# Second stage's transfers issued from GpSimd's queue, first stage's layer 0 spread over all tiles, third stage's groups started one after another

## The chip, the cores and the metric

The kernel runs on one core of a Trainium2 chip. The core has five engines that run beside each other, each through its own list of instructions in order: TensorE (PE; its weight loads are listed as PEld), VectorE (DVE), ScalarE (ACT), GpSimd (POOL) and SyncE (SP), which computes nothing and issues transfers. Data lies in HBM (DRAM), in SBUF, and the results of matmuls in PSUM. The metric is the device time of one execution in microseconds (us); lower is better. Before the change it is 4272.32 us, the median of three runs (4270.29 to 4274.1).

## What is computed

Four graph layers run over 128 graphs of 128 nodes with 128 channels; each adds its result to x. `LN` is a layer normalisation over the channels, followed by a ReLU.

```python
h = relu(LN(x));  x = x + L0(h, adj)   # relation-typed mean of neighbours, norm, relu
h = relu(LN(x));  x = x + L1(h, adj)   # learned adjacency, below
h = relu(LN(x));  x = x + L2(h, adj)   # graph attention, 4 heads of 32
h = relu(LN(x));  x = x + L3(h, adj)   # graph attention, 1 head, elu
```

The costly part is layer 1, which looks at every pair of nodes of a graph:

```python
D = abs(x[:, :, None, :] - x[:, None, :, :])        # all pairs i, j
h = einsum('bijc,oc->bijo', D, W1) + b1             # 64 features a pair
h = (h - mean(h)) / sqrt(var(h) + EPS) * g1 + be1   # mean, var over ALL graphs and pairs
s = einsum('bijo,uo->biju', leaky(h), W2)[..., 0] + b2[0]
A = softmax(where(adj > 0, s, NEG), axis=-1)
y = einsum('bij,bjc->bic', A, x) @ Wg.T + bg
y = leaky(batchnorm(y))                             # again over all graphs
out = concatenate([x, y], axis=2) @ Wt.T + bt
```

The two normalisations over all graphs cut the work into three stages: no score can be computed before the features of all pairs are known, and no output before all y.

## The kernel before

Work is done in 32 groups of G = 4 graphs. The partitions are the nodes (or, for pair features, 2 x 64 features).

**Stage 1** does layer 0 and the pair features. `pairs(g)` takes a group's transposed `h`, and `pair_stats` goes through four tiles (`t`) of each of its four graphs (`k`), so a group has 16 tiles. For a tile, `pairwise` subtracts (line 164, output `d`; tiles 0 and 2 on DVE, 1 and 3, which are those in `ON_POOL`, on GpSimd), ACT takes the absolute value (166), PE multiplies with `w1T` (170, output `hp`), ACT copies to `hs` (182), and DVE takes statistics (183 to 190). `hs` goes to DRAM per graph (188). There are two `d` tiles for each of the two engines and two `hp` tiles. `layer0(g + 2)` runs beside `pairs(g)`: it is a generator of 13 pieces (loads; statistics; mask and degrees, lines 238 to 244; norm; two transposes; matmuls; sum; statistics; scale, 278; shift and add to x, 284, stored by 285; statistics; the norm for layer 1), each of the three norms with a power on GpSimd (116, 117). `_weave(main, side, steps)` takes `steps` pieces of the side work for each step of the main work, and what is left of it at the end. A program builder then orders the instructions of each engine by its own estimate, starting from the order in which the code issues them, and puts in the waits.

**Stage 2** reads the stored pair features back as z in halves of a graph, 1 MiB each (`fetch`, line 485; ten are fetched ahead, twelve buffers). `scores` normalises them (507 and 512 on ACT, 508 on DVE), multiplies by W2 (503) and copies out (519); `by_k` finishes a graph's scores (525, 529, 531) into `sk`. `to_rows` writes `sk` to a DRAM buffer `rows` with a skewed layout (538) and loads it back as `u` (541), which turns diagonals into rows. `finish1` loads x (547), normalises it (129, 140, output `hn`), transposes it (146), adds the two halves of u (556), does the softmax (555 to 574) and the matmuls (581 to 593), stores the new x (590) and y (596, into Z). In the loop, group g's scores run beside `finish1(g - 2)`. All of these transfers are issued from SP's queue, so one that waits for its data holds those behind it.

**Stage 3** does the rest of layer 1 and layers 2 and 3 per group (`group`, 30 steps): load (729 on), a first product (740), a norm, attention for two graphs at a time (757 to 762 into `pe`, softmax 690 to 700, transposes 146, product 777), a norm, layer 3's attention (795 to 812), store (820). Its tiles have three buffers, `x` four, `e` eight. `_round_robin` keeps three groups under way: it fills up to three, and gives each one step per turn. Since all groups have the same number of steps, three start together and end together.

Of the kernel before, what the change touches and what calls it, by code (L numbers as in the profile page):

```python
# [30 lines left out]
AHEAD = 2  # L31
# [9 lines left out]
def _weave(main, side, steps):  # L41


    due = 0.0
    for _ in main:
        due += steps
        while due >= 1:
            due -= 1
            next(side, None)
    for _ in side:  # L50
        pass


def _round_robin(works, at_once):

    flying = []
    while True:
        flying += list(itertools.islice(works, at_once - len(flying)))
        if not flying:
            return  # L60
        flying = [w for w in flying if next(w, works) is not works]


# [1 line left out]
def tile_gnn_stack(ctx: ExitStack, tc: tile.TileContext, a: dict, out: bass.AP):  # L65
    nc = tc.nc
    NB = a["x"].shape[0]
    NG = NB // G
# [6 lines left out]
    def big(name):  # L75
        return psum.tile([P, 2, 512], F32, tag="big", bufs=2, name=name)

    def sm(name):
        return psum.tile([P, G, P], F32, tag="sm", bufs=3, name=name)
# [23 lines left out]
    X = [dr.tile([P, G, P], F32, tag=f"x{g}", name=f"x{g}") for g in range(NG)]  # L103
    Z = [dr.tile([P, G, P], F32, tag=f"z{g}", name=f"z{g}") for g in range(NG)]
# [38 lines left out]
    def transpose(dst, src, func=AF.Copy):  # L143
        pt = sm("pt")
        for k in range(G):
            nc.tensor.transpose(pt[:, k, :], src[:, k, :], ident)  # L146
        nc.scalar.activation(dst, pt, func)  # L147

    def over_group(t):
        return t[:, None, :].to_broadcast([P, G, P])  # L150
# [42 lines left out]
    with tc.tile_pool(name="c0", bufs=1) as c0, tc.tile_pool(name="p0", bufs=2) as p0:  # L193
# [97 lines left out]
        def pairs(g):  # L291

            h = H1.pop(g)
            xp = psum.tile([P, G, P], F32, tag="xp", name="xp")
            for k in range(G):
                nc.tensor.transpose(xp[:, k, :], h[:, k, :], ident)
            xe = p0.tile([P, G, P + 2 * KH], F32, name="xe")
            nc.scalar.copy(xe[:, :, 0:P], xp)
            nc.scalar.copy(xe[:, :, P:], xp[:, :, 0:2 * KH])
            for k in range(G):  # L300
                yield from pair_stats(p0, xe, xp, k, g * G + k)
# [49 lines left out]
        with tc.If(nc.values_load(flag, min_val=0, max_val=1) > 0) as cmp, \  # L351
# [6 lines left out]
            for g in range(NG):  # L358
                x = pr.tile([P, G, P], F32, name="x")
# [36 lines left out]
            pass  # L396

        for g in range(NG):
            _weave(pairs(g), layer0(g + AHEAD) if g + AHEAD < NG else iter(()), 4)


    with tc.tile_pool(name="bn", bufs=1) as bn:
# [39 lines left out]
    with tc.tile_pool(name="c1", bufs=1) as c1, tc.tile_pool(name="p1", bufs=2) as p1:  # L442
# [26 lines left out]
        zero = c1.tile([P, G, ROW], F32, name="zero")  # L469
        nc.vector.memset(zero, 0.0)  # L470
        for n in range(2):
            rows = dr.tile([G, P, ROW], F32, tag=f"rows{n}", name=f"rows{n}")
            nc.sync.dma_start(rows.rearrange("g i r -> i g r"), zero)
            slots.append(rows)

        sk = []
# [11 lines left out]
        def next_z():  # L488
            z = fetched.pop(0)
            n = next(halves, None)  # L490
            if n is not None:
                fetched.append(fetch(n))
            return z

        def scores(k, s):

            ps = big("ps")[:, 0, :]

            def products(parts, j0):
                for i, (w, v) in enumerate(parts):  # L500
                    for c in range(4):
                        w0 = 31 - 2 * (j0 // 4)
                        nc.tensor.matmul(ps[32 * c:32 * c + 32, :], w[:, w0:w0 + 32], v[:, 512 * c:512 * c + 512],  # L503
                                         start=j0 == 0, stop=j0 > 0 and i == 1, skip_group_check=True)

            z0 = next_z()
            nc.scalar.activation(z0, z0, AF.Identity, bias=bias1, scale=scale1[:, 0:1])  # L507
            nc.vector.scalar_tensor_tensor(z0, z0, 0.01, z0, op0=OP.mult, op1=OP.max)  # L508
            yield
            z1 = next_z()  # L510
            zr = p1.tile([P, NT // 2 * KC * P], F32, name="zr", bufs=3)
            nc.scalar.activation(zr, z1, AF.Relu, bias=bias1, scale=scale1[:, 0:1])  # L512
            products([(w2z, z0)], 0)

            if behind:
                behind.pop()()
            products([(w2l, z1), (w2r, zr)], 4)
            su = p1.tile([P, 4, P], F32, name="su")
            nc.vector.tensor_copy(su.rearrange("p a b -> p (a b)"), ps)  # L519
            yield  # L520

            def by_k():
                pk = sm("pk")
                for kk in range(4):
                    nc.tensor.matmul(pk[:, kk, 0:16], su[:, kk, :], pick.rearrange("p h j -> p (h j)"),  # L525
                                     start=True, stop=True)

                out_k = s[:, k, 1:].rearrange("p (a b) -> p b a", b=4)
                nc.vector.tensor_tensor(out_k, pk[:, :, 0:16], add_k.rearrange("p h j -> p (h j)")[:, None, :]
                                        .to_broadcast([P, 4, 16]), OP.add)  # L530
                nc.vector.tensor_scalar(s[:, k, 2 * KH:], s[:, k, 2 * KH:], 0.5, None, op0=OP.mult)
            behind.append(by_k)

        def to_rows(g):

            rows = slots[g % 2]
            to = rows[0, 0, 0:1]
            nc.sync.dma_start(bass.AP(tensor=to.tensor, offset=to.offset,
                                      ap=[[ROW + 1, P], [P * ROW, G], [1, 1 + 2 * KH]]), sk[g % 2])
            u = p1.tile([P, G, ROW], F32, name="u")  # L540
            nc.sync.dma_start(u, rows.rearrange("g i r -> i g r"))
            return u

        def finish1(g, u):

            x = p1.tile([P, G, P], F32, name="x")
            nc.sync.dma_start(x, X[g])
            yield
            h = pre_norm(p1, x, MV1[:, g], RS1[:, g])
            yield  # L550
            hT = p1.tile([P, G, P], F32, name="hT")
            transpose(hT, h)
            yield
            cap = p1.tile([P, G, P], F32, name="cap")
            nc.vector.tensor_scalar(cap, M8[g], BIG, NEG12, op0=OP.mult, op1=OP.add)
            nc.vector.tensor_tensor(u[:, :, 0:2 * KH], u[:, :, 0:2 * KH], u[:, :, P:], OP.add)
            yield
            pt = sm("put")
            for k in range(G):
                nc.tensor.transpose(pt[:, k, :], u[:, k, 0:P], ident)  # L560
            yield
            e = p1.tile([P, G, P], F32, name="e1")
            nc.vector.tensor_tensor(e, u[:, :, 0:P], pt, OP.add)
            nc.vector.tensor_tensor(e, e, cap, OP.min)
            mx = small.tile([P, G], F32, name="mx")
            nc.vector.tensor_reduce(mx, e, AX.X, OP.max)
            yield
            nc.vector.tensor_tensor(e, e, mx[:, :, None].to_broadcast([P, G, P]), OP.subtract)
            nc.scalar.activation(e, e, AF.Exp)
            yield  # L570
            sums = small.tile([P, G], F32, name="sums")
            nc.vector.tensor_reduce(sums, e, AX.X, OP.add)
            nc.vector.reciprocal(sums, sums)
            nc.vector.tensor_tensor(e, e, sums[:, :, None].to_broadcast([P, G, P]), OP.mult)
            yield
            aT = p1.tile([P, G, P], F32, name="aT")
            transpose(aT, e)
            yield
            py = sm("py")
            for k in range(G):  # L580
                nc.tensor.matmul(py[:, k, :], h[:, k, :], aT[:, k, :], start=True, stop=True)
            yT = p1.tile([P, G, P], F32, name="yT")
            nc.scalar.copy(yT, py)
            yield
            po = sm("po")
            for kk in range(G):
                nc.tensor.matmul(po[:, kk, :], hT[:, kk, :], wtxT, start=True, stop=True)
            nc.vector.tensor_tensor(x, x, po, OP.add)
            nc.vector.tensor_tensor(x, x, over_group(bt), OP.add)
            nc.sync.dma_start(X[g], x)  # L590
            yield
            pz = sm("pz")
            nc.tensor.matmul(pz, wgT, yT, start=True, stop=True)
            y = p1.tile([P, G, P], F32, name="y")
            nc.scalar.activation(y, pz, AF.Identity, bias=bg)
            nc.sync.dma_start(Z[g], y)
            nc.vector.bn_stats(ST2[:, g, :], y.rearrange("p a b -> p (a b)"))

        def group_scores(g):
            for k in range(G):  # L600
                yield from scores(k, sk[g % 2])

# [25 lines left out]
    with tc.tile_pool(name="c2", bufs=1) as c2, tc.tile_pool(name="p2", bufs=3) as p2:  # L630
# [188 lines left out]
            nc.vector.scalar_tensor_tensor(x, ex, 1.0, x, op0=OP.min, op1=OP.add)  # L819
            nc.sync.dma_start(out[g * G:g * G + G].rearrange("b t c -> t b c"), x)  # L820

        _round_robin((group(g) for g in range(NG)), 3)


# [29 lines left out]
```

## Time and profile before

The profiled execution took 4268.02 us from the host's view of the device; its span, from the first to the last instruction, is 4266.1 us. The mean TensorE clock granted was 0.805.

| | PE | PEld | DVE | ACT | GpSimd |
|---|---|---|---|---|---|
| busy, us | 2964.6 | 1531.3 | 2913.5 | 2624.5 | 1419.4 |
| share of the span | 69% | 36% | 68% | 62% | 33% |

| stage | from, us | to, us | what marks it |
|---|---|---|---|
| 1 | 100 | 2101 | first and last `hp` matmul, line 170 |
| 2 | 2108 | 3215 | first fetch of z, line 485, to the sums over all y, line 621 |
| 3 | 3217 | 4266 | first `off`, line 736, to the end |

A row of busy times by window gives the window and its length, then for each engine the busy time and in brackets the number of instructions, then the granted clock of TensorE (1 is full speed), the busy share of the 16 transfer engines and GB/s. A row of waits gives the engine and the line that waited, what ended the wait, the total in us, the number of times and the longest. A timeline row gives start, duration, engine (SPq is SP's queue), line, operation, tiles, count, and in square brackets the idle time before it and what ended that.

In the whole profile every transfer but four runs through one queue, SP's, with 652 MB; no transfer is issued from GpSimd. `z<-hp` is 256 issues of 1 MiB with a median of 11.9 us to landing, `u<-rows` 5.6 us, `rows<-sk` 3.4 us, `x<-x` (loads and stores of all stages) 4.3 us.

### The profile page before, as it was taken

To read this page: it belongs to the slowest core of one execution; us is meant where nothing else is said; L and a number is where in the kernel's file an instruction comes from. 1 tells how busy PE (TensorE), PEld (TensorE's weight loads), DVE (VectorE), ACT (ScalarE), POOL (GpSimd) and SP (SyncE) were. 2 spreads that over 40 slices of the span, in tenths; PEclk is the share of its full clock that TensorE was granted. 3 is DMA by queue.
4 is the path that set the end of the run, shared out by engine and by line. 5 is a ranking of instruction groups with operands and counts; after the bars stand their busy time and mean duration, and the time that the engine had idled before them with its cause. 6 is when DMAs were issued, how large, how long until landed. Compare 5 with 4: busy or idle time off the path is not lost.

```text
span 4266.1 us, 43744 instructions
## 1 busy us (share of the span) xinstructions
PE 2964.6 (69%) x15142; PEld 1531.3 (36%) x15153; DVE 2913.5 (68%) x5971; ACT 2624.5 (62%) x3363; POOL 1419.4 (33%) x683
## 2 busy tenths in 40 slices
PE   1566666666657667666677677777777888888887
PEld 1222222222222222222123343333445666666665
DVE  5888888888888888877646666666665555555544
ACT  1677777777777777777755555555544554555544
POOL 2566666666666666556400000000001111111111
PEclk7788788888888878878877777777777888888877
DMA  6343333333333333333577777777751001000000
GB/s 205 121 170 156 136 156 155 133 158 153 143 148 153 153 138 153 150 128 160 220 295 288 298 303 294 278 289 302 305 183 45 23 29 39 23 23 23 21 16 15
DMA packets 182965, 659.12 MB, mean 155 GB/s; under 512 B 31312, under 2 KB 99792, under 8 KB 132560
## 3 DMA queue, kind: packets, MB, share of 16 engines
q1 hardware_dynamic: 182160, 652.04, 39.9%
q10 hardware_dynamic: 576, 4.19, 0.3%
q8 instruction: 123, 2.02, 0.2%
q14 instruction: 106, 0.87, 0.1%
HBM read 340.76 MB, written 315.42 MB: 154 GB/s over the span
## 4 chain that ended last, share of the span: by engine, by line
PE 42%; ACT 25%; DVE 10%; POOL 9%; DMA 7%; issue 5%; SPq 0%; POOLq 0%; DVEq 0%; ACTq 0%
PE hp L170 14%; ACT d L166 13%; POOL d L164 9%; ACT hs L182 6%; PE ps L503 5%; DMA x<-x 4%; PE pt L146 4%; PE pv L777 4%; PE pk L525 3%; PE pe L759 3%; DVE z L508 3%; PE pe L757 3%; DMA rows<-sk 2%; ACT e L700 2%; PE pr L718 2%
## 5 line engine op out<-in xcount | busy, mean ns | idle before, releaser
L170 PE MATMUL hp<-d,w1T 128*64 128x512 f32 x4096 | 1146.3, 706 | 691.4 <-ACT d L166 686.1
L164 POOL TENSOR_TENSOR d<-xe 128x2048 f32<-128x2048 f32 x256 | 1081.9, 4243 | 500.5 <-PE hp L170 463.9
L166 ACT ACTIVATE d<-d 128x2048 f32<-128x2048 f32 x512 | 968.7, 1921 | 307.3 <-POOL d L164 299.4
L170 PEld LDWEIGHTS hp<-d,w1T 128*64 128x64 f32 x4096 | 314.2, 161 | 1439.8 <-ACT d L166 862.3
L182 ACT COPY hs<-hp 128x1024 f32<-128x1024 f32 x512 | 516.1, 1021 | 216.6 <-PE hp L170 216.4
L164 DVE TENSOR_TENSOR d<-xe,xp 128x2048 f32<-128x2048 f32 x256 | 579.9, 2275 | 84.2 <-PE hp L170 84.2
L183 DVE BATCH_NORM_STATS2 st<-hs 128x6 f32<-128x512 f32 x512 | 350.0, 684 | 192.2 <-ACT hs L182 189.5
L507 ACT ACTIVATE z<-z,bias,scale 128x2048 f32<-128x2048 f32 x128 | 267.4, 2089 | 202.9 <-DMA z<-hp 191.2
L116 POOL TENSOR_SCALAR scale<-mv 128x1 f32<-128x1 f32 x1 | 0.2, 226 | 1106.7 <-DVE mv L621 1106.7
L116 POOL TENSOR_SCALAR lnrs<-lnmv 128x4 f32<-128x4 f32 x128 | 34.6, 270 | 962.9 <-DVE lnmv L124 962.9
L512 ACT ACTIVATE zr<-z,bias,scale 128x2048 f32<-128x2048 f32 x128 | 267.7, 2092 | 103.8 <-DMA z<-hp 71.4
L185 DVE BATCH_NORM_STATS2 st<-hs 128x6 f32<-128x512 f32 (+1 forms) x512 | 327.8, 640 | 0.0
L700 ACT ACTIVATE e<-e,mx 128x128 f32<-128x128 f32 x640 | 248.5, 392 | 86.1 <-DVE mx L697 84.8
L508 DVE SCALAR_TENSOR_TENSOR z<-z 128x2048 f32<-128x2048 f32 x128 | 292.3, 2285 | 12.3 <-ACT z L507 12.3
L147 ACT ACTIVATE hT<-pt 128x512 f32<-128x512 f32 x128 | 78.9, 616 | 325.4 <-PE pt L146 325.3
L691 DVE TENSOR_REDUCE mx<-e 128x4 f32<-128x512 f32 x160 | 104.7, 682 | 197.9 <-ACT e L690 196.7
L503 PE MATMUL ps<-z,w2z 128*32 128x512 f32 x1024 | 186.9, 812 | 56.6 <-DVE su L519 27.3
L146 PE MATMUL pt<-ident,e 128*128 128x128 f32 x768 | 150.7, 312 | 58.5 <-ACT e L700 23.0
L525 PEld LDWEIGHTS pk<-pick,su 128*128 128x128 f32 x1024 | 174.7, 256 | 37.5 <-DVE su L519 21.0
L777 PE MATMUL pv<-wr,eT 128*128 128x32 f32 x1024 | 168.0, 322 | 27.7 <-ACT eT L147 16.8
L146 PE MATMUL pt<-ident,hn 128*128 128x128 f32 x256 | 61.0, 358 | 179.5 <-DVE hn L140 179.5
L503 PE MATMUL ps<-z,w2l 128*32 128x512 f32 x1024 | 182.2, 794 | 0.4 <-DMA z<-hp 0.4
(190 smaller groups left out, 4784.2 us busy)
## 6 DMA issues: line engine op xcount, KB each, us to landing
hp<-hs SPq DMA_DIRECT2D x128, 2048.0 KB, 6.3
z<-hp SPq DMA_DIRECT2D x256, 1024.0 KB, 11.9
x<-x SPq DMA_DIRECT2D x128, 256.0 KB, 4.3
u<-rows SPq DMA_DIRECT2D x32, 384.0 KB, 5.6
x<-in_x_dram SPq DMA_DIRECT2D x32, 256.0 KB, 2.8
adj<-in_adj_dram SPq DMA_DIRECT2D x32, 256.0 KB, 4.6
agg<-a SPq DMA_DIRECT2D x32, 256.0 KB, 2.7
z<-y SPq DMA_DIRECT2D x32, 256.0 KB, 3.6
```

Source lines behind the costliest of these rows:

```text
L146: nc.tensor.transpose(pt[:, k, :], src[:, k, :], ident)
L164: eng.tensor_tensor(d, ahead, x[:, None, None, :].to_broadcast([P, 2, KC, P]), OP.subtract)
L166: nc.scalar.activation(d, d, AF.Abs)
L170: nc.tensor.matmul(hp[64 * hh:64 * hh + 64, c:c + 512], w1T, d[:, hh, c:c + 512], start=True, stop=True)
L182: nc.scalar.copy(hs[:, t, :], hp)
L183: nc.vector.bn_stats(st[:, 2 * t, :], hs[:, t, 0:512])
L185: nc.vector.bn_stats(st[:, 2 * t + 1, :], hs[:, t, 512:1024 - P * last])
L503: nc.tensor.matmul(ps[32 * c:32 * c + 32, :], w[:, w0:w0 + 32], v[:, 512 * c:512 * c + 512], start=j0 == 0, stop=j0 > 0 and i == 1, skip_g ...
L508: nc.vector.scalar_tensor_tensor(z0, z0, 0.01, z0, op0=OP.mult, op1=OP.max)
L525: nc.tensor.matmul(pk[:, kk, 0:16], su[:, kk, :], pick.rearrange("p h j -> p (h j)"), start=True, stop=True)
L700: nc.scalar.activation(e[:, q, :], e[:, q, :], AF.Exp, bias=mx[:, t, q:q + 1], accum_out=sums[:, t, q:q + 1])
L777: nc.tensor.matmul(pv[:, k - k0, hd, :], eT[:, hd, :], wr[:, k, 32 * hd:32 * hd + 32], start=True, stop=True)
```

## The change

Three things are edited.

1. `_weave` in stage 1 takes 0.75 steps of `layer0` per tile instead of 4. A group has 16 tiles, so 12 of the 13 pieces are taken within it and the last one after it.
2. In stage 2 the filling of `rows` with zeros, the store of `sk`, the load of `u`, the load and the store of x and the store of y are issued from GpSimd's queue (`nc.gpsimd.dma_start`). The fetches of z stay on SP's.
3. In stage 3 `_round_robin(..., 3)` becomes `_staggered(..., 10)`: a new group is started every ten turns, and all groups under way get one step per turn.

```diff
-def _round_robin(works, at_once):
+def _staggered(works, gap):

-    flying = []
+    flying, turn = [], 0
     while True:
-        flying += list(itertools.islice(works, at_once - len(flying)))
-        if not flying:
-            return
+        if turn % gap == 0 or not flying:
+            flying += list(itertools.islice(works, 1))
+            turn = 0
+            if not flying:
+                return
+        turn += 1
         flying = [w for w in flying if next(w, works) is not works]
...
-            _weave(pairs(g), layer0(g + AHEAD) if g + AHEAD < NG else iter(()), 4)
+            _weave(pairs(g), layer0(g + AHEAD) if g + AHEAD < NG else iter(()), 0.75)
...
-            nc.sync.dma_start(rows.rearrange("g i r -> i g r"), zero)
+            nc.gpsimd.dma_start(rows.rearrange("g i r -> i g r"), zero)
...
-            nc.sync.dma_start(bass.AP(tensor=to.tensor, offset=to.offset,
+            nc.gpsimd.dma_start(bass.AP(tensor=to.tensor, offset=to.offset,
                                       ap=[[ROW + 1, P], [P * ROW, G], [1, 1 + 2 * KH]]), sk[g % 2])
...
-            nc.sync.dma_start(u, rows.rearrange("g i r -> i g r"))
+            nc.gpsimd.dma_start(u, rows.rearrange("g i r -> i g r"))
...
-            nc.sync.dma_start(x, X[g])
+            nc.gpsimd.dma_start(x, X[g])
...
-            nc.sync.dma_start(X[g], x)
+            nc.gpsimd.dma_start(X[g], x)
...
-            nc.sync.dma_start(Z[g], y)
+            nc.gpsimd.dma_start(Z[g], y)
...
-        _round_robin((group(g) for g in range(NG)), 3)
+        _staggered((group(g) for g in range(NG)), 10)
```

## The prediction

> **What bounds the kernel now.** The kernel is three stages with barriers of data between them, so I cut the span first. The 40-slice rows and the first and last starts of the source-line view give stage 1 (lines 170 and below) to 2101 us, stage 2 (lines 485 to 597) to about 3215, stage 3 to 4266. Then I asked each stage for its busy time by window and for its waits.
>
> Stage 1: a window over one group of 128 `hp` matmuls each. The first line is a group that has a `layer0` woven in, the last two are the final groups, which have none left.
>
> ```profile
> 700.00:764.00 64.00, 41.96 (x168) 14.30 (x166) 52.14 (x99) 46.40 (x38) 40.16 (x16) 0.80 0.37 146
> 2003.00:2052.00 49.00, 33.37 (x132) 9.01 (x132) 38.44 (x52) 44.12 (x34) 32.92 (x9) 0.90 0.40 172
> 2052.00:2101.00 49.00, 32.01 (x130) 8.34 (x128) 39.10 (x53) 44.03 (x33) 33.33 (x8) 0.93 0.41 172
> ```
>
> [...]A group without `layer0` takes 49 us and ACT is 90% busy in it (44.1). With it a group takes 63.3 us on average (the fourth `hp` store of a group, line 188, leaves at 167.7 for the first group and at 2003.6 for the thirtieth: 1835.9 / 29) although no engine is over 83% busy: DVE gained 13.4 us of work and the group got 14 us longer. The work is added end to end, not beside.
>
> Stage 2, waits between 2250 and 3100 us, which are 25 groups:
>
> ```profile
> ACT z L507 <- DMA z<-hp: 168.0, 25, 7.9
> PE pt L146 <- DVE hn L140: 164.1, 26, 8.0
> DVE sk L529 <- PE pk L525: 132.5, 102, 2.8
> DVE u L556 <- DMA u<-rows: 129.2, 25, 6.4
> ```
>
> and of the queue SP alone:
>
> ```profile
> SPq L590 <- DVE x L589: 530.5, 25, 21.7
> ```
>
> Once per group ACT (for z), PE (for hn) and DVE (for u) all stand for 5 to 8 us. The SP line says why the fetches of z are late: for 21 us of each group SP stands at the store of line 590, with the fetches behind it. The timeline of one group shows the burst that follows:
>
> ```profile
> 2504.14 0.32 SPq L590 DMA_DIRECT2D x<-x  x1
> 2506.24 0.37 SPq L538 DMA_DIRECT2D rows<-sk  x1
> ...
> 2509.89 0.37 SPq L541 DMA_DIRECT2D u<-rows  x1
> 2510.32 0.50 SPq L547 DMA_DIRECT2D x<-x  x1
> 2510.86 4.46 SPq L485 DMA_DIRECT2D z<-hp  x7
> ...
> 2514.96 0.42 DVE L556 TENSOR_TENSOR u<-u 128x256 f32<-128x256 f32 x1 [4.70 <-DMA u<-rows]
> ...
> 2519.43 1.09 PE L146 MATMUL pt<-ident,hn 128*128 128x128 f32 x4 [5.53 <-DVE hn L140]
> ```
>
> The load of x (547) also stands behind line 541, which waits 3.6 us for `rows` to land. The period is about 33.2 us (line 538 at 2506.24, 2538.82, and so on over the stage).
>
> Stage 3: the timeline of SP (stores of three groups together), and a window over one such round.
>
> ```profile
> 4089.60 3.38 SPq L820 DMA_DIRECT2D out_dram<-x  x3
> 4184.21 3.38 SPq L820 DMA_DIRECT2D out_dram<-x  x3
> 4261.34 1.77 SPq L820 DMA_DIRECT2D out_dram<-x  x2
> ```
>
> ```profile
> 3380.00:3475.00 95.00, 78.30 (x448) 60.94 (x448) 51.38 (x156) 48.00 (x163) 12.49 (x15) 0.84 0.08 26
> ```
>
> Three groups in step take 95.5 us, the final two 74.1 (to 4261.3 from 4187.2, where the last store of the round before was issued). So one more group costs 21.4 us and 31 us per round are latency that all three stand through together. PE's waits in that round (`pt` for `h`, two of 4.3 and 5.3 us) are the normalisations, which all three reach at once. PE is at a mean clock of 0.84.
>
> [...] the windows around 5 to 8 us gaps show 0.50 and transposes take 1.09 us instead of 0.63.
>
> **Part by part.** The order in which the changed program's instructions stand was read beside the order of before; durations are those of before.
>
> *Layer 0 spread (4 to 0.75 steps per tile).* Nothing is added. In DVE's order the 14 us of `layer0` work, which stood in the first quarter of a group, now stand in two lumps of 6 to 8 us, and ACT's order alternates `d` and `hs` through two thirds of the group instead of half. Floor: DVE's 52.1 us. The undisturbed groups run at 90% of their busiest engine; 52.1 / 0.90 = 57.9 us. 63.3 - 57.9 = 5.4, over 30 groups 162 us. Ends: 11.2 x 30 = 336 (DVE never waits), and 0, or a loss of 2 us a group if GpSimd, where the power of the normalisation queues behind a 4.2 us `d`, holds DVE longer, three times per group, than the 75.2 us in 27 groups that the waits from 200 to 1900 us show (2.8 a group).
>
> *Second stage on GpSimd's queue.* GpSimd is idle there (its row shows 0 in slices 21 to 30). Per group five DMAs leave SP: rows, u, x, X, Z; SP keeps eight z fetches, which wait only for their slot. In DVE's account a group is 21.0 busy + 5.2 (u) + 5.3 (pk) + 1.1 (po) + 0.8 (rest) = 33.4. After: (a) x is now issued ahead of the wait for rows, and `hn` stands one group ahead of the transposes that use it, so PE's 6.3 us wait goes, and with it the half clock after it. DVE's wait for pk exists because PE is late; I take 2.0 of 5.3 as left (DVE still outruns PE at the fourth tile). (b) z is no longer behind line 590: ACT's 6.7 us wait goes. (c) u is late next: it still follows sk, rows and its own landing. Before it landed 8.9 us after sk[...]. On GpSimd the X and Z transfers stand between, but while rows lands. DVE's order has 6.0 us of work in that time (before 3.8): wait 3.7 instead of 5.2. Sum 33.2 - 3.3 - 1.5 = 28.4 us, 4.8 x 30 = 144 us. Ends: DMA share 0.78 of 33 is 25.8 us of full DMA, so at most 7.4 x 30 = 222; the other end is the slower rival. What GpSimd computes in stage 3 (powers, `off`) is behind the last stores only.
>
> *Third stage staggered.* The diff also starts a group every 10 steps instead of three together. A group has 30 steps, so three still fly, with the same buffers. PE's work at full clock: 95.5 less 11.3 of gaps is 84.2; about 24 of the 30 us at half clock are busy and save 12; 72.2 / 3 = 24.1 us per group. Floor 24.1, now 31.9. In the changed order PE still waits for a softmax and a norm per group, but others' matmuls stand between, so waits are hops of 1 to 2 us and the clock stays up. I take 28.0 (4 us of hops). The last group runs out alone, about 65 us (53 = 31 + 21.4, with company at first): 31 x 28.0 + 65 = 933 against 10 x 95.5 + 74.1 = 1029: 96 us. Ends: 24.1 gives 217, and 32 gives a loss of 28.
>
> Sum: 162 + 144 + 96 = 402. The profiled execution took 4268.0 (span 4266.1), so 3866; the median stands 4.3 above it: 3870.
>
> **Rivals.**
> 1. Layer 0 gives nothing: DVE's waits move to GpSimd's queue. For: 2.8 us of such waits exist. Against: the use now stands two tiles after. 4268 - 240 + 4 = 4032.
> 2. Stage 2 gives nothing: u with its two serial landings still sets the period, since it is the one path that the change lengthens. 4268 - 258 + 4 = 4014.
> 3. All three come near their floors (54, 26.5 and 25.5 us): 279 + 201 + 176 = 656, 3616. Against it: engines in order never pack so well in before.
> 4. Slower: [...] At 6 us per transfer u lands 4 x 6 + 4 = 28 us after sk, DVE stands at line 556 22.0 us instead of 3.7: 46.7 us a group, +13.5 x 30 = 405, less 258 of the other stages: 4419. It decides from 4.8 us per transfer on. For it: rows and u are 512 pieces each of 260 and 768 bytes, and no row shows such a DMA. [...]
>
> **How the numbers follow.** Forecast 0.54, rivals 1 to 4: 0.13, 0.13, 0.10, 0.07; nothing moves 0.03. Range 3690 to 4060: holds the forecast's spread (two of three terms off by half, 150 us) and rivals 1 and 2, leaves out 3 and 4. 0.2% (8.5 us) is about what a measurement tells. Faster 0.90 (forecast, 1, 2, 3), same 0.02, slower 0.08.
>
> **What would show it.** Stage 1: distance of the stores of line 285 near 58, PE gaps under 4 us. Stage 2: no wait of z on DMA, SP never at a store, period of rows near 28, a DVE wait for u of 3 to 4 us[...]. Stage 3: stores evenly 28 us apart and a clock near 1. A u landing later than 16 us after sk, or a stage 1 group over 62, would make it wrong.

## The result and the profile after

The changed kernel takes 4400.01 us (median of 4 runs, 4390.66 to 4422.48), the kernel before 4273.21 us in the same comparison: a ratio of 1.0304, with an interval of 1.0264 to 1.0344. It is about 127 us slower, where 402 us less had been forecast. The profiled execution has a span of 4400.9 us against 4266.1.

Cut at the same marks as before:

| stage | before, us | after, us | difference | forecast |
|---|---|---|---|---|
| 1 | 2000 | 1982 | -18 | -162 |
| 2 | 1117 | 1258 | +141 | -144 |
| 3 | 1049 | 1061 | +12 | -96 |

**Stage 1.** The row of busy times of the same window as before, from the changed kernel:

```profile
700.00:764.00 64.00, 40.74 (x168) 13.58 (x164) 60.19 (x101) 46.88 (x38) 39.78 (x17) 0.87 0.36 148
```

DVE's busy time went from 52.14 to 60.19 us, although the diff adds no instruction. Most of its waits are gone as forecast, but it works longer: it is busy for 94% of the window, and a group still takes 63.2 us (63.4 before; mean distance of the fourth `hp` stores, groups 4 to 27 of both traces).

**Stage 2.** The period, from one issue of `rows` to the next, is 38.4 us (33.2 before). DVE's waits between 2250 and 3100 us, which are now 22.1 groups:

```profile
DVE u L559 <- DMA u<-rows: 138.2, 22, 7.7
DVE su L522 <- PE ps L506: 108.2, 66, 3.9
DVE hn L132 <- DMA x<-x: 61.2, 23, 6.9
DVE sk L532 <- PE pk L528: 50.0, 22, 2.3
```

No ACT wait for z is left among the waits of that window (before: 168.0 us). In its place come `su` for the products (4.9 us per group) and `hn` for x (2.8 us), and the wait for u grew from 5.2 to 6.2 us. The landings (issue, number of transfers, KB each, median us to landing), first in that window, then between 3250 and 3335 us, where the last fetch of z is past:

```profile
u<-rows POOLq DMA_DIRECT2D x23, 384.0 KB, 8.4
...
rows<-sk POOLq DMA_DIRECT2D x22, 130.0 KB, 6.4
```

```profile
u<-rows POOLq DMA_DIRECT2D x2, 384.0 KB, 3.6
rows<-sk POOLq DMA_DIRECT2D x2, 130.0 KB, 4.0
```

On the same queue u lands in less than half the time, and `rows` in 4.0 us instead of 6.4, once no z is fetched beside them. In one group's timeline DVE shows what this costs:

```profile
2510.25 0.15 DVE L534 TENSOR_SCALAR sk<-sk 128x1 f32<-128x1 f32 x1
...
2526.78 0.43 DVE L559 TENSOR_TENSOR u<-u 128x256 f32<-128x256 f32 x1 [7.73 <-DMA u<-rows]
```

In this group u is used 16.4 us after `sk` (15.7 in the median of groups 5 to 27 of the trace), not the 9.7 that the forecast's 6.0 of work and 3.7 of wait come to.

**Stage 3.** Stores, and the busy row of 750 us, of the changed kernel:

```profile
3804.66 0.39 SPq L825 DMA_DIRECT2D out_dram<-x  x1
...
3835.49 0.39 SPq L825 DMA_DIRECT2D out_dram<-x  x1
...
3866.27 0.39 SPq L825 DMA_DIRECT2D out_dram<-x  x1
...
3900.13 0.39 SPq L825 DMA_DIRECT2D out_dram<-x  x1
```

```profile
3500.00:4250.00 750.00, 622.07 (x3591) 468.89 (x3589) 406.21 (x1244) 388.64 (x1316) 98.55 (x120) 0.92 0.08 25
```

The groups do leave one by one, but 31.6 us apart on average (30.8 three times, then 33.9), where three in step took 95.5 / 3 = 31.8.

### The profile page after: what moved, and what is told of

The parts are those of the page before. It is cut to its first block, busy times and chain, and to the rows that moved or that the text cites. A ratio compares the mean times of both kernels' runs of the same rounds, so it can differ in the third digit from the quotient of the medians.

```text
span 4400.9 us, 43943 instructions
## 1 busy us (share of the span) xinstructions
PE 3003.8 (68%) x15153; PEld 1479.3 (34%) x15153; DVE 3145.9 (71%) x5971; ACT 2618.1 (59%) x3363; POOL 1508.0 (34%) x845
## 3 DMA queue, kind: packets, MB, share of 16 engines
q10 hardware_dynamic: 576, 4.19, 0.2%
## 4 chain that ended last, share of the span: by engine, by line
PE 34%; DVE 33%; ACT 10%; DMA 10%; issue 7%; POOL 6%; SPq 0%; POOLq 0%; ACTq 0%; DVEq 0%
PE ps L506 7%; DVE d L167 6%; DMA u<-rows 5%; PE hp L173 4%; DVE st L186 4%; DMA rows<-sk 4%; DVE hn L132 4%; DVE st L188 3%; ACT d L169 3%; DVE o L281 3%; PE pv L782 3%; POOL d L167 3%; PE pe L762 3%; PE pe L764 3%; DVE mask L241 2%
## 5 line engine op out<-in xcount | busy, mean ns | idle before, releaser
L173 PE MATMUL hp<-d,w1T 128*64 128x512 f32 x4096 | 1161.7, 705 | 462.2 <-ACT d L169 345.7
L169 ACT ACTIVATE d<-d 128x2048 f32<-128x2048 f32 x512 | 992.1, 1938 | 349.2 <-DVE d L167 206.5
L173 PEld LDWEIGHTS hp<-d,w1T 128*64 128x64 f32 x4096 | 301.4, 159 | 1216.0 <-ACT d L169 570.6
L528 PE MATMUL pk<-pick,su 128*128 128x16 f32 x1024 | 156.7, 287 | 310.1 <-DVE su L522 310.1
L593 POOL DMA_DIRECT2D x<-x x32 | 17.3, 541 | 849.5 <-DVE x L592 818.8
L528 PEld LDWEIGHTS pk<-pick,su 128*128 128x128 f32 x1024 | 149.5, 221 | 425.7 <-DVE su L522 411.4
L695 ACT COPY e<-pe 128x512 f32<-128x512 f32 x160 | 90.6, 589 | 300.3 <-PE pe L767 255.4
L132 DVE TENSOR_SCALAR hn<-x,MV,RS 128x128 f32<-128x128 f32 x256 | 195.3, 827 | 93.9 <-DMA x<-x 83.9
L572 ACT ACTIVATE e<-e 128x512 f32<-128x512 f32 x32 | 20.2, 630 | 366.6 <-DVE e L571 366.6
L149 PE MATMUL pt<-ident,e 128*128 128x128 f32 x768 | 191.1, 324 | 57.7 <-ACT e L705 37.9
```

The source lines that it names most:

```text
L132: nc.vector.tensor_scalar(dst[:, k, :], src[:, k, :], mv[:, k, 0:1], rs[:, k:k + 1], op0=OP.subtract, op1=OP.mult)
L169: nc.scalar.activation(d, d, AF.Abs)
L173: nc.tensor.matmul(hp[64 * hh:64 * hh + 64, c:c + 512], w1T, d[:, hh, c:c + 512], start=True, stop=True)
```

## Experiments

### Each edit alone

e1 has edit 2 alone, e2 has edit 1 and e3 has edit 3, each with the lines of the change.

> The kernel before with edit 2 alone (stage 2's transfers on GpSimd's queue). Theory A, the whole loss of the change comes from stage 2 because rows and u land late there: 4273 + 125 to 140 = 4400 to 4415, group period 38 us, u landing 16 us after sk, DVE standing 6 us per group at the add of u. Rival, the loss needs the three edits together (stage 1 or stage 3 slower in company): 4250 to 4300.

> The kernel before with edit 1 alone (layer 0 at 0.75 steps per tile). If [...] (DVE's short layer 0 operations are stretched beside GpSimd's 4.2 us subtraction, busy time instead of waits): 4245 to 4265, DVE busy above 90% of stage 1. If the gain that was forecast is there and only hidden in company: 4111 (162 us less).

> The kernel before with edit 3 alone (a group of stage 3 every ten steps). From the trace of the changed kernel stage 3 is as long as before: 4265 to 4295, clock of stage 3 near 0.92 and one PE wait of 3.5 us for a norm per group. If the forecast of stage 3 holds alone: 4177.

| kernel | median, us | ratio | interval |
|---|---|---|---|
| e1 | 4416.82 | 1.0351 | 1.0332 to 1.0371 |
| e2 | 4244.74 | 0.9949 | 0.9936 to 0.9962 |
| e3 | 4281.66 | 1.0035 | 1.0021 to 1.0048 |

Against 4265.96 these are +151, -21 and +16, in sum +146; the change itself has +127. The edits nearly add up, and the loss is edit 2's. In e2 DVE is busy for 1641.7 us between 130 and 1860 us, as in the change (1641.3).

### Stage 2: which transfer?

e4 moves only x and y, e5 only rows and u.

```diff
-            nc.sync.dma_start(x, X[g])
+            nc.gpsimd.dma_start(x, X[g])
...
-            nc.sync.dma_start(X[g], x)
+            nc.gpsimd.dma_start(X[g], x)
...
-            nc.sync.dma_start(Z[g], y)
+            nc.gpsimd.dma_start(Z[g], y)
```

> The kernel before with only the load of x, the store of x and the store of y on GpSimd's queue; the zero filling, the store of sk to rows and the load of u stay on SP. Theory A (the two serial landings of rows and u on GpSimd's queue set the period): rows and u land as before or later by what SP's fetches ahead of them cost, z no longer stands behind the store of x, stage 2 is 60 to 150 us shorter than before: 4125 to 4215. Rival B (the load of x, which waits on GpSimd's queue for the store of x, or the changed order of instructions, costs the time): still slow, 4370 to 4410.

4390.73 us (1.0297, 1.0277 to 1.0318): as slow as the whole change, with rows and u where they were. Theory A, that their landing on GpSimd's queue is the whole loss, fell here; in this kernel DVE has no wait for u to speak of. Nor does the run tell the two halves of B apart (the load of x behind its store, or the order): the builder had put the instructions of PE, DVE and ACT into another order than in the kernel before. PE took the products of one graph at a time instead of two graphs back to back, so DVE's `su` waits for PE and PE's `pk` waits for `su`.

> The kernel before with only rows and u (lines 473, 538, 541) on GpSimd's queue. In this one the builder keeps the order of PE and ACT as before, and that of DVE but for a few places. Theory A (rows and u land late on GpSimd's queue, 6.4 and 8.3 us instead of 3.4 and 5.6): DVE stands 5.7 us longer per group at the add of u, 4266 + 32 x 5.7 = 4450. Theory C (the loss comes from the builder's new order of instructions, not from the queue): 4240 to 4300.

4462.59 us (1.0446, 1.0428 to 1.0463), near the 4450 of A, and with the old order almost untouched (29 of DVE's 1069 instructions of stage 2 stand elsewhere). Two causes, then, and they had to be separated.

### Stage 2: the queue and the order, one at a time

In e7 to e9 every instruction of PE, DVE and ACT in stage 2 has an edge (`NoSync`) to the one before it in a list, `ORDER`, that was read out of another kernel's built program. What these edges cost by themselves was not run.

```diff
+def _pin(tc, order):
+    named = {i.name: i for i in tc.nc.cur_bb.bb.instructions}
...
+        for one, then in zip(row, row[1:]):
+            tc.add_manual_dep(then, one.name, mybir.DependencyInfo(
+                mybir.DependencyClass.NoSync, mybir.DependencyReason.DATA), reason="order")
...
             _weave(main, side, 1.5)
+        _pin(tc, ORDER)
```

> Edit 2 alone (all of stage 2's transfers on GpSimd's queue), with PE, DVE and ACT held in stage 2 to the order that they have in the kernel before. Theory C (order): the loss of 151 us is gone, 4150 to 4290. Theory A (late landings on GpSimd's queue): still 4390 or more, since DVE reaches the add of u as early as before.

> The kernel before with every transfer on SP's queue as it was, with PE, DVE and ACT held in stage 2 to the order that edit 2 gives them. Theory C (order): slow without any GpSimd transfer, 4390 to 4450, su waiting for ps and PE for su as in the changed kernel. Theory A (queue): 4250 to 4290.

> Only the load of x and the stores of x and y on GpSimd's queue (as in e4_xyz_on_gpsimd, 4391), with PE, DVE and ACT held in stage 2 to the order of the kernel before. Theory C (order): z no longer stands behind the store of x, and nothing else is later: 4120 to 4240. Rival B (the load of x waiting on GpSimd's queue for the store of x): 4370 to 4410.

| transfers of stage 2 | old order | new order (that of e1) |
|---|---|---|
| all on SP | 4271.94 (before) | 4487.03 (e8: 1.0515, 1.0475 to 1.0556) |
| all on GpSimd | 4375.92 (e7: 1.0238, 1.0221 to 1.0255) | 4416.82 (e1: 1.0351, against 4265.96) |
| x and y on GpSimd | 4289.79 (e9: 1.0041, 1.0026 to 1.0055) | 4390.73 (e4: 1.0297, in its own order) |

The traces confirm the lists: by operation and tile, PE, DVE and ACT run stage 2 in e7 and e9 (and in e14 and e17 below) in exactly the order of before, and in e8 in that of e1.

Both causes are real and they don't add up. With the old order held, the queue costs 104 us (e7); with SP's queue held, the order costs 215 (e8). Along the other two sides of the table, the new order costs 41 us on GpSimd's queue (e1 against e7), and in the new order GpSimd's queue is 70 us faster than SP's (e1 against e8; e1 is from another comparison, whose kernel before was 6 us faster). So neither has one price, and no theory had the sizes: e7 and e9 fell between the two ranges expected, e8 above both. e9 does answer the other half of B: with the load of x behind the store of x on GpSimd's queue the old order loses 18 us, not the 125 of e4.

In e7, DVE and PE between 2250 and 3100 us, 23 groups:

```profile
PE pt L168 <- DVE hn L162: 249.4, 23, 13.0
DVE u L578 <- DMA u<-rows: 216.6, 23, 10.8
```

DVE stands 9.4 us per group for u (before: 5.2), and what is behind it on DVE (`hn`) makes PE stand 10.8 (before: 6.3). In e8 it is `hn` that stands, 11.0 us per group:

```profile
DVE hn L151 <- DMA x<-x: 231.9, 21, 13.5
```

It stands for a load of x that SP issues behind the load of u, which waits for `rows` to land, and behind two fetches of z. The 215 us are thus the price of this order on this queue.

e9 shows why freeing z brought nothing. In it SP doesn't store x any more, but it stands just as long at rows, with the fetches behind it (SP's waits, 25 groups):

```profile
SPq L560 <- DVE sk L553: 599.5, 25, 24.3
```

Only e7 frees SP, and ACT's wait for z is gone there, but DVE and PE stand for u instead. The old order also explains why u is always waited for. The code keeps `finish1` a group behind, but the builder moved it up: in DVE's order between the `sk` that goes into the rows of one `u` and the add of that same `u` stand only the first `sk` of the next group, two `su`, one z and a `bn_stats`.

### Why u lands late

> As e7_gpsimd_old_order (4376), with 6 buffers of z instead of 12, so that at most 4 to 5 fetches of 1 MiB are in flight, not 10. Contention theory (u lands late because z is fetched without a break beside it): with fewer fetches in flight u lands in 4 to 6 us instead of 8.3, and the time falls by 30 to 100, to 4275 to 4345. Queue theory (GpSimd's queue is slow in itself): u still lands in about 8 us, and the time stays at 4376 or rises, as z comes later.

```diff
-            z = p1.tile([P, NT // 2 * KC * P], F32, name="z", bufs=FETCHED + 2)
+            z = p1.tile([P, NT // 2 * KC * P], F32, name="z", bufs=6)
```

4443.19 us (1.0414, 1.0388 to 1.0440), and u still lands in 8.1 us, as the queue theory expected. But the edit hardly did what it was meant to: by the issues and landings in the traces, 2.7 fetches were on their way when u was issued in e7, and 2.0 in e14 (means of groups 5 to 27). The wider comparison is with e5: 6.9 were on their way there, and u landed in 8.3 us. So the number in flight makes little difference. e17 puts rows and u on ACT's queue, in the old order, to see whether u is late on any queue but the one that fetches z; the profile of e17 lists ACT's queue (q10) as hardware_dynamic like SP's (q1), and GpSimd's (q0) as software_dynamic.

> As e7_gpsimd_old_order, with rows and u issued from ACT's queue[...]; the load of x and the stores of x and y stay on GpSimd, the old order is held. The landing of u is the measure. Queue theory (GpSimd's software queue is slow): u lands in 4 to 6 us and rows in 3 to 4. Sharing theory ([...]): u lands in 7 us or more. The time, with ACT standing at rows and u: 4300 to 4450, and it decides nothing.

The time is 4473.90 us (two runs); DVE stands 13.3 us per group for u (266.4 us in 20 groups). The landings between 2250 and 3050 us, then between 3290 and 3400, at the end of the fetches:

```profile
u<-rows ACTq DMA_DIRECT2D x19, 384.0 KB, 13.1
...
rows<-sk ACTq DMA_DIRECT2D x19, 130.0 KB, 4.2
```

```profile
u<-rows ACTq DMA_DIRECT2D x4, 384.0 KB, 3.4
```

The late landing doesn't need GpSimd's queue: u is late on either second queue (13.1 us on ACT's, 8.3 on GpSimd's in e7) as long as fetches of z run in the first. `rows` lands in 4.2 us in e17; it is issued when only one fetch is left on its way. The packets in the traces show where u's time goes (us from the issue of u; means of groups 5 to 27, or of the last groups, where no fetch is left):

| u in | its packets | first and last one start after | packets of z between them |
|---|---|---|---|
| before, SP | 512 of 768 bytes | 2.5, 5.2 | 51 |
| e17, ACT | 512 of 768 bytes | 3.7, 12.5 | 338 |
| e17, ACT, last 3 groups | 512 of 768 bytes | 1.1, 2.9 | 0 |
| e5, GpSimd | 112, mean 3.5 KB | 4.0, 7.8 | 136 |
| e5, GpSimd, last 2 groups | 112, mean 3.5 KB | 1.5, 3.2 | 0 |

In the kernel before, u was issued on SP ahead of the burst of seven fetches, and few of their packets (51) come between its own. From a second queue the same 512 packets are mixed with 338. In 512 small packets on ACT's queue u took longer to land (13.1 us) than in 112 larger ones on GpSimd's (8.3 in e5), with 136 of z between them. How the packets come to be mixed was not shown: the traces don't name the transfer engine of a packet.

### Stage 2 with an order of its own

e11 is e1 with an order written by hand: products of graph b, then `pk` of b - 1, with z of b + 1 normalised ahead, the load of x beside that of u, and `finish1` a whole group behind its u. e12 is the change with the same.

```diff
+            z0, z1, zr = ready.pop()
+            if b + 1 < NB:
+                ready.append(halves_of())
             products([(w2z, z0)], 0)
...
-            return u
-
-        def finish1(g, u):
-
             x = p1.tile([P, G, P], F32, name="x")
             nc.gpsimd.dma_start(x, X[g])
-            yield
+            return u, x
+
+        def finish1(g, u, x):
+
...
+        latest = {}
+        for i in nc.cur_bb.bb.instructions[start:]:
...
+                    tc.add_manual_dep(i, latest[i.engine], mybir.DependencyInfo(
+                        mybir.DependencyClass.NoSync, mybir.DependencyReason.DATA), reason="order")
```

> Edit 2 alone (all of stage 2's transfers on GpSimd's queue), with an order for PE, DVE and ACT written by hand: each graph's z is normalised one graph ahead of its use, the load of x moves to the place of the load of u, and finish1 stays a whole group behind, so u has some 25 us to land. Theory D (the late landing costs only because the add of u stands right behind the sk it comes from): no wait for u or x, period 26 to 29 us, 4272 - 32 x (33.2 - 27.5) = 4090, in 4040 to 4160. Theory A alone (GpSimd's queue too slow for these transfers): 4370 to 4420 whatever the order.

> The changed kernel (all three edits) with the same hand-written order in stage 2. Theory D: about 5 us less than e11_order_by_hand (stage 1 gives 21, stage 3 takes 16): 4085, in 4035 to 4155. Theory A alone: 4370 to 4410.

4283.71 (1.0026, 1.0017 to 1.0035) and 4277.91 us (1.0016, 1.0008 to 1.0023): the loss is gone, all on GpSimd's queue, but both missed the gain. DVE's wait for u is gone too, and another has its place:

```profile
DVE z L500 <- ACT z L497: 283.1, 99, 6.0
```

That is 11.3 us per group: in ACT's order the scaling of the next z stands behind the softmax and the copies of the transposes, which wait themselves (the longest, for DVE's `e`, 111.8 us in 25 groups). e16 (edits 1 and 2) scales z two graphs ahead and puts each piece of `finish1` a part of a group behind the one it depends on.

```diff
+            z0, z1, zr = ready.pop(0)
+            if b + 2 < NB:
+                ready.append(scaled(b + 2))
+            if b + 1 < NB:
+                leaky(ready[0][0])
```

> Edits 1 and 2 with a hand-written order in stage 2 in which ACT scales z two graphs ahead and DVE finishes it one graph ahead, and each piece of finish1 that PE or ACT takes from DVE stands a part of a graph later. Theory D (only the order keeps the gain of edit 2 away): no wait of DVE for ACT's z, period 26 to 29 us, 4245 - 32 x (33.2 - 27.5) = 4060, in 4010 to 4130. If sharing the transfer engines sets the period (z at 1 MiB times 8 per group beside the rest): period 31 to 33, 4200 to 4260.

4157.17 us (0.9737, 0.9720 to 0.9753), slower than the range expected. The period is 30.7 us, below the 33.2 of before though not the 26 to 29 expected; DMA share 0.86. What sets the 30.7 was not pursued; DVE's longest wait there is for `pk` (213.1 us in 24.4 groups). u lands in 8.3 us as in the changed kernel, and nobody waits for it. So a late landing costs nothing if the order leaves u its time. How much of the gain belongs to the queue stays open: the same order with every transfer on SP's queue was not run.

### Stage 1: DVE beside GpSimd's subtractions

> Edit 1 alone with all d tiles on DVE, none on GpSimd (ON_POOL empty). [...] (DVE's short layer 0 operations last several times longer when GpSimd subtracts beside them): line 129 falls from about 1.3 us in the weave to 0.4, line 238 from 3.8 to 0.8, line 278 from 1.3 to 0.5, although DVE is busier than ever. Rival (they last longer because of transfers or of ACT's traffic): they stay as long. The time itself rises by 100 to 400 us, as DVE takes over 8 subtractions of 2.27 us per group.

```diff
-ON_POOL = {1, 3}
+ON_POOL = set()
```

4669.96 us (1.0933, 1.0906 to 1.0960). DVE's groups between 130 and 1860 us (count, busy us, mean ns), of the changed kernel and of e10:

```profile
L281 DVE SCALAR_TENSOR_TENSOR o<-o,lnmv,gamma 128x128 f32<-128x128 f32 x112 | 145.9, 1341 | 0.0
L132 DVE TENSOR_SCALAR hn<-x,MV,RS 128x128 f32<-128x128 f32 x109 | 138.8, 1332 | 6.8 <-POOL RS L120 6.8
L241 DVE TENSOR_SCALAR mask<-adj 128x512 f32<-128x512 int32 x27 | 102.5, 3798 | 0.0
```

```profile
L129 DVE TENSOR_SCALAR hn<-x,MV,RS 128x128 f32<-128x128 f32 x92 | 26.9, 342 | 12.1 <-POOL RS L117 12.1
L278 DVE SCALAR_TENSOR_TENSOR o<-o,lnmv,gamma 128x128 f32<-128x128 f32 x92 | 26.7, 344 | 0.0
...
L238 DVE TENSOR_SCALAR mask<-adj 128x512 f32<-128x512 int32 x22 | 9.0, 409 | 0.0
```

Without GpSimd's 4.2 us subtractions beside them the same instructions take about a quarter of the time or less. The trace of the changed kernel shows one of them beside a subtraction:

```profile
753.08 4.19 POOL L167 TENSOR_TENSOR d<-xe 128x2048 f32<-128x2048 f32 x1 [2.15 <-PE hp L173]
...
753.76 3.79 DVE L241 TENSOR_SCALAR mask<-adj 128x512 f32<-128x512 int32 x1
```

The subtraction ends at 757.27 us and `mask` 0.28 us later. All 27 of `mask`, 28 of 109 `hn` and 50 of 112 `gamma` are stretched between 130 and 1860 us, and each of these 105 ends a fixed time after a GpSimd subtraction: 0.28 us, 0.08 us and 0.15 us, to within 0.01 us. Of DVE's own subtractions (one input in PSUM) 92 began beside one of GpSimd's, and of the statistics of lines 186 to 190 435; none of them is stretched. So the price shows as busy time, not as a wait, and falls on certain instructions alone; why on these was not shown. e19, on top of e18 (below), tests whether a stretched instruction lasts until the end of one subtraction, or is as long whenever GpSimd subtracts.

```diff
-        eng = nc.gpsimd if on_pool else nc.vector
-        eng.tensor_tensor(d, ahead, x[:, None, None, :].to_broadcast([P, 2, KC, P]), OP.subtract)
+        if on_pool:
+            for c in range(0, KC, 2):
+                nc.gpsimd.tensor_tensor(d[:, :, c:c + 2, :], ahead[:, :, c:c + 2, :],
+                                        x[:, None, None, :].to_broadcast([P, 2, 2, P]), OP.subtract)
+        else:
+            nc.vector.tensor_tensor(d, ahead, x[:, None, None, :].to_broadcast([P, 2, KC, P]), OP.subtract)
```

> As e18_best, with each of GpSimd's subtractions in stage 1 cut into four of a quarter of the size. [...] (a stretched DVE operation lasts until GpSimd's instruction ends): lines 238 to 278 wait for a quarter of the hold, mask falls from 3.8 to about 1.3 us, hn and gamma from 1.34 to about 0.6; 8 us less DVE time in a group, of which stage 1 gains 3 to 8 over 30 groups: 90 to 240 below e18_best. If [...]: mask and hn stay as long, and the time is within 20 us of e18_best or above it.

3746.15 us (0.8766, 0.8751 to 0.8780), 142 below e18. A group of stage 1 takes 58.0 us instead of 63.2. DVE's instructions in e19 between 130 and 1600 us:

```profile
L132 DVE TENSOR_SCALAR hn<-x,MV,RS 128x128 f32<-128x128 f32 x100 | 102.8, 1087 | 0.0
L285 DVE SCALAR_TENSOR_TENSOR o<-o,lnmv,gamma 128x128 f32<-128x128 f32 x104 | 99.1, 991 | 0.0
L289 DVE SCALAR_TENSOR_TENSOR o<-o,lnrs,beta 128x128 f32<-128x128 f32 x104 | 78.5, 813 | 0.0
L245 DVE TENSOR_SCALAR mask<-adj 128x512 f32<-128x512 int32 x25 | 19.8, 793 | 0.0
```

`mask` falls from 3802 ns in e18 to 793. `hn` (from 1313) and `gamma` (from 1361) fall less, and `beta` rises from 340: each stretch is short, the longest of these instructions takes 1.28 us, but more of them are stretched. In e18 23 of 92 `hn`, one in a group of four, are stretched, in e19 all 100. The expected size for these was wrong, the direction right. A part of the 142 may be the order that the builder made of the smaller pieces.

### Stage 3: how many groups are under way

> As e12_all_by_hand, with PE, DVE and ACT held in stage 3 too to the order in which the code issues the staggered groups. If the builder's order keeps the staggered groups in step at their waits: stage 3 goes from about 1060 to 930 to 1000 us, 60 to 130 below e12. If the waits come from the chain of operations of a group itself: within 20 us of e12, or above it.

4618.89 us (1.0813, 1.0793 to 1.0834), 341 above e12: it decides little, since the order of the code is far worse than the builder's there (PE waits 181.3 us for `e` in 1100).

> As e3_stagger_only (4282; a group of stage 3 every 31.5 us), with a group started every 8 steps instead of 10, so that four are under way, and one more buffer for its tiles. Theory L (a group takes about 93 us from start to end in company, and three under way give 31): the distance of the stores falls to 25 to 28 us, 4282 - 32 x 4.5 = 4140, in 4090 to 4190. Theory H (PE's hops of 3.5 us at the norms and the softmax set it, whatever is under way): 4260 to 4300.

```diff
-        _round_robin((group(g) for g in range(NG)), 3)
+        _staggered((group(g) for g in range(NG)), 8)
...
-    with tc.tile_pool(name="c2", bufs=1) as c2, tc.tile_pool(name="p2", bufs=3) as p2:
+    with tc.tile_pool(name="c2", bufs=1) as c2, tc.tile_pool(name="p2", bufs=4) as p2:
```

(`x` has 5 buffers instead of 4, `e` 10 instead of 8, `eT` 8 instead of 6.) 4009.15 us (0.9390, 0.9373 to 0.9407), 265 us faster from stage 3 alone. Its busy row, and PE's longest total wait, between 3400 and 3900 us:

```profile
3400.00:3900.00 500.00, 484.83 (x3317) 388.55 (x3316) 368.69 (x1142) 351.51 (x1208) 96.06 (x110) 1.00 0.11 33
```

```profile
PE pt L149 <- DVE h L132: 6.8, 10, 0.7
```

PE is 97% busy at full clock, and stores leave 22.6 us apart. Theory L has the direction and undersized the gain (4090 to 4190 expected). In the traces a group takes 88 us from its first product to its store in the changed kernel and 77 in e15, so more company didn't lengthen its way. An estimate from these traces: three groups bring 3 x 22 = 66 us of work for PE, less than the 88 that one takes, and four bring 88. The fourth group and the buffers came together; which of the buffers it needs, and whether they alone would help, was not run.

### All together

> The three edits of the change, with stage 2's order of e16_two_ahead and stage 3 of e15_four_flying (a start every 8 steps, four buffers). If the stages add up as before: 4157 + 4009 - 4273 = 3893, in 3870 to 3915.

3888.29 us (0.9097, 0.9082 to 0.9112), against 3893 from the sum: the three stages add up. With e19's cut in stage 1 it is 3746.15 us, 12% below the kernel before and the fastest of all.

## Why the prediction was wrong

The sign was wrong, and each of the three terms failed, at a step that can be named.

**Layer 0 spread: "Nothing is added."** True of instructions, false of time. The floor of 52.1 us was taken from durations in an order in which fewer of DVE's instructions were stretched beside GpSimd's subtractions (1 of 112 `hn` and 25 of 108 `gamma`, against 28 of 109 and 50 of 112) and `mask` less (825 ns on average, against 3798). Between 130 and 1860 us DVE's busy time rose from 1422.6 to 1641.3 us, some 8 us a group, and ate the wait that went. The trace of before already had the signs, where e10 has 682 and 409 ns:

```profile
L284 DVE SCALAR_TENSOR_TENSOR x<-o,x 128x512 f32<-128x512 f32 x27 | 66.5, 2464 | 0.0
L238 DVE TENSOR_SCALAR mask<-adj 128x512 f32<-128x512 int32 x27 | 22.3, 825 | 0.0
```

I took DVE's durations over as they stood and didn't ask which of them change with what GpSimd does beside them. With shorter subtractions (e19) the group takes the 57.9 us of the forecast by coincidence: DVE is 98% busy there, not for 52.1 us. Rival 1 had nearly the size (nothing; e2 shows 21 us) by another mechanism: DVE's waits for GpSimd didn't grow but fell, to 6.8 us in 27 groups.

**Stage 2, items (a) and (b) as to what goes.** The waits of PE for `hn` and of ACT for z went, and DVE's wait for `pk` is 2.3 us where 2.0 was said. GpSimd's time to issue is 0.54 to 0.76 us, far under the 4.8 from which rival 4 decides: that its 4419 lies near the 4400 measured is luck.

**Stage 2, item (c), and the account as a whole.** u was expected 9.7 us after `sk`, where 8.9 had been measured; the 0.8 between them was my estimate, which no trace showed. It is 16.4. The step that failed is that the landings of before were carried over: they were measured with u ahead of the fetches on one queue. The change frees SP, so fetches run on another queue beside u (e5, e17, and the landings of 3.4 to 3.6 us without fetches). Rival 2 said that this is the path which the change lengthens; it had 0.13. Then the account kept two lines too few: `su` 4.9 and `hn` 2.8 us per group, waits that stand in the order that the builder made anew. I had read that order for what it gained (`hn` a group ahead) and not for what it lost (two graphs' products back to back). With u's 2.5 us more (6.2 instead of 3.7) they are 10.2, and 28.4 + 10.2 = 38.6, against 38.4 measured. e7 and e8 show that the new queue in the old order, or the new order on the old queue, suffices to turn the gain of 144 into a loss.

**Stage 3: "waits are hops of 1 to 2 us and the clock stays up".** The clock rose only to 0.92, PE is busy 26.2 us a group (622.07 / 750 x 31.6) instead of 24.1, as much as before (78.30 / 3 = 26.1) although the clock rose, which stays open, and stands 5.4 instead of 4. What failed was to sum PE's work and take three groups under way as enough to cover a group's latency; "three still fly" was in the text, with no question what three can cover. e15 shows what a fourth group with its buffers is worth. The floor of 24.1 was also too high: the row of before shows PE busy 78.30 of 95 us, so idle for 16.7 and not 11.3, and (78.3 - 12) / 3 = 22.1, where e15 has 21.9. (The third term of rival 3 comes to 174 by its own sum, not 176.)

## What to carry over

When a wait of a queue is removed, ask what that wait held back: here SP's standing (530.5 us in 25 groups) kept the fetches behind the transfer on the critical path. Read also what order the builder makes of the changed program, since that is a change of its own. Give a transfer that must land its time in the order of the instructions (u a group behind) before changing the queue it goes through. Starting groups one by one, without more of them under way, moves the waits apart and leaves the latency (31.6 us a group here, 31.8 before): count groups times work per group against the latency of one.

## What the runs showed of the hardware

- In the changed kernel a transfer issued from GpSimd held that engine for 0.54 us (256 KB of x) or 0.76 us (rows, u). The landing of u went with what ran in other queues: 8.4 us beside fetches and 3.6 without (changed kernel); on ACT's queue 13.1 and 3.4 (e17); on SP's own queue, ahead of the fetches, 5.7 (before). Whether 2.0 or 6.9 fetches were on their way made no such difference (8.1 in e14 and 8.3 in e5).
- A DVE instruction of 0.41 us on 512 elements (`mask` in e10) took 3.80 us on average beside GpSimd subtractions of 4.19 us (changed kernel), where it ended 0.28 us after the subtraction each time, and 0.79 beside those of 1.20 us (e19), all of it counted as busy.
- PE at full clock (1.00, e15) needs 22 us for a group of stage 3 (484.83 / 500 x 22.6 = 21.9); at a mean of 0.92 (changed kernel) it was busy for 26.2.
